# Two-layer graph attention on one core: the second layer's hub rows computed between the layers, 36 row tiles, waits by tile, a shorter norm pipeline

## The chip, the cores and the metric

The kernel runs on one core of one Trainium2 chip. The metric is device time in microseconds (us); lower is better. Three runs of the kernel before gave a median of 1045.44 us (1041.41 to 1046.57).

## The reference, cut to what matters

Eight batches of 2048 nodes with 64 features pass a two-layer graph attention net, are added to the input and normalised. An edge mask, the same for all batches and heads, decides which nodes attend to which.

```python
mask = graph + jnp.eye(N) > 0                    # N = 2048
h = jnp.einsum('bnc,hdc->bhnd', x, Wh)           # 4 heads, D = 64
out_h = softmax(where(mask, h @ h.T, -1e16)) @ h + bh     # layer 1, per head
z = leaky_relu(cat(out_h), 0.2)
h2 = jnp.einsum('bnk,dk->bnd', z, Wo)
out2 = softmax(where(mask, h2 @ h2.T, -1e16)) @ h2 + bo   # layer 2
z2 = leaky_relu(out2, 0.2)
y = layernorm(z2) * gamma + beta
return layernorm(x + y)
```

## The kernel before, in words

The mask is sparse: on average few neighbours, many only for low node numbers. The kernel (`fast_kernel`) therefore splits the nodes. The first 56 are hubs and attend densely to all nodes. The other 1992 form 166 sets of 12 nodes; each set gets a list of up to 128 nodes to which any of its members is linked, built from the mask (`make_keys`, `pick`). An indirect DMA on GpSimd (`gather`, L792) fetches the 128 rows of a set, 520 floats each, from a table in DRAM. All instructions are recorded in the order of the Python code; each engine runs its own in that order, and waits on semaphores for the others. No scheduler moves anything.

The work has three stages.

Stage one (to about 165 us) builds hub attention of layer 1, the key lists and table1.

Stage two is a loop over `i` in units of two sets (83 units) for layer 1. In one unit PE transposes the gathered rows of a later unit (`turn`, L512) into a PSUM tile that ScalarE copies to `xTg` (L1030), computes scores (L821), multiplies the weights by the values (`values`, L846), transposes the result (L863), projects it through the heads (L531), then through Wo into layer-2 columns (L880), and transposes these to rows (L890). `keep_own` (L885, L886) stores the columns as `own`, `keep_rows` (L894) stores rows and SyncE writes them to table2 (L897). The last unit's table2 rows are complete only at the end of the loop.

Stage three is layer 2, a loop over `u` in units of four sets (42 units, the last with two), on new pools `late` and `psum2`. Every gather of layer 2 reads table2, so none can begin before all its rows are written. 24 row tiles let the gathers of six units go ahead. In unit `u` the code issues, in this order: the scores of unit u+2 (`scores2`, L1133, and their exp on ScalarE, L1136); the value products of u (`values2`, L1165) into `op`, a PSUM tile for two units; on some units the value products of a hub block (L1299); the gathers of u+6; the jobs of running norms (`work_on(u, 0)`); the square roots of the norms (`roots`, L1239 and L1240); the weights of a hub block (L1285, L1288); the block-diagonal queries of u+3 (`spread_own`, L1124); the transposed scores of u+1 (L1144) and their mask (L1152); the transposes of u+4 (`turn2`, L512, and the copies L1320); the scores of a hub block (L1277); the remaining norm jobs (`work_on(u, 1)`).

The dense attention of the 56 hubs in layer 2 has 18 blocks (17 of up to 120 keys and one with the hubs themselves). Each costs a DMA of its rows (`hub_block`, L1267), eight score matmuls (L1277), a mask on VectorE (L1285), an exp on ScalarE (L1288) and 16 value matmuls (L1299). Four of them are in units -4 to -1, the other 14 in every second unit from 2 to 28.

A finished pair of units gives one norm (`norm`), 21 in all and one for the hubs. Its steps are: divide by the row sums (`first`, L1186 and L1188), leaky relu (L1193), sum (L1197), centre (L1202) and squares on ScalarE (L1204), sum of squares (L1213), root on ScalarE, scale, gamma and residual (`again`, L1217, L1221, L1222), then sum, centre, squares, sum of squares, root, scale again (`end`), and eight stores (L1248). The list that `norm` returns spreads them over eight units:

```python
return [([], [first, act, mean(0)]), ([centre(0)], []), ([var(0)], []), ([], [again, mean(1)]), ([centre(1)], []),
        ([], []), ([var(1)], []), ([end], [])]
```

At the end a flag is written which says whether the sums stayed in range; every engine loads it, and a general kernel would run if it were set.

Of the kernel before, what the change touches and what calls it, by code (L numbers as in the profile page):

```python
# [359 lines left out]
def fast_kernel(ctx: ExitStack, tc: tile.TileContext, x, adj, Wh, bh, Wo, bo, gamma, beta, out, flag):  # L360
# [54 lines left out]
    wnat = early.tile([P, H, C], F32, name="wnat")  # L415
    whT = early.tile([P, H * D], F32, name="whT")
    gram = early.tile([P, H, P], F32, name="gram")
    wos = early.tile([D, H * D], F32, name="wos")
# [68 lines left out]
    number = early.tile([P, 2, HALFN], U16, name="number")  # L487
# [81 lines left out]
    yh = early.tile([P, 2, 2 * HUB * H], F32, name="yh")  # L569
# [52 lines left out]
    def hub_later(t, new):  # L622
# [4 lines left out]
        def turn_back():  # L627
            pt = new(f"oth{t}", "T")
            for v in range(2):
                for k in range(2):  # L630
                    nc.tensor.transpose(pt[:, 0, (2 * v + k) * P:(2 * v + k + 1) * P], osb[:, v, k, :], ident)
            ot = held["oth", t] = work.tile([P, H, n], F32, tag="ot", name=f"otbh{t}")
            nc.scalar.copy(ot.rearrange("c h (w n) -> c h w n", w=8),
                           pt[:, 0, :].rearrange("c (w n) -> c w n", w=8)[:, :, :HV].rearrange("c w (n h) -> c h w n", h=H))
# [28 lines left out]
    keys = [early.tile([P, HALFN], F32, name=f"keys{k}") for k in range(2)]  # L663
    cand = early.tile([P, SEG * KEEP], F32, name="cand")
    best = early.tile([P, P], F32, name="best")
# [61 lines left out]
    def pick(r):  # L727
# [32 lines left out]
        def slots():  # L760
            nc.vector.tensor_copy(over[:, 2 * r + 1:2 * r + 2], best[:, P - 1:P])
            pb = two(f"pb{r}") if r == 0 else late_two(f"pb{r}")
            nc.tensor.transpose(pb[:, 0, :P], best, ident)
            for c, a, n in runs:
                nc.vector.tensor_copy(keysi[:, a:a + n], pb[:, 0, c:c + n])
            nc.vector.tensor_scalar(index[:, s0:s0 + n_r], keysi[:, s0:s0 + n_r], N - 1, None, OP.bitwise_and)
# [125 lines left out]
    def keep_rows(g, pr):  # L892
# [3 lines left out]
        for j in range(2):  # L896
            nc.sync.dma_start(out=dst[2 * g + j], in_=r[j * 48:(j + 1) * 48])  # L897
# [105 lines left out]

    begin = ExitStack()
    psum1 = begin.enter_context(tc.tile_pool(name="psum1", bufs=1, space=bass.MemoryType.PSUM))
# [4 lines left out]
    def late_two(name):  # L1010
        return one(name, "T")
# [5 lines left out]
    for i in range(-4, NG + 3):  # L1017
# [6 lines left out]
        cat = one(f"cat{i}", "C")  # L1024
# [3 lines left out]
        if 0 <= i + 2 < NG:  # L1028
            t = held["T", 1, i + 2] = work.tile([P, 2, 512], F32, tag="xTg", name=f"xTg{i + 2}", bufs=3)
            nc.scalar.copy(t, held.pop(("tp", i + 2)))  # L1030
# [6 lines left out]
        if 0 <= i + LOOK < NG and i > -3:  # L1037
            for j in range(2):
                gather(table1, 2 * (i + LOOK) + j, 1, rows_tile)
        if i + 6 < NG and i % 2 == 0 and i >= -2:  # L1040
            own_rows((i + 6) // 2)
        if 0 <= (i - 30) // 2 <= NV:
# [18 lines left out]
        if 0 <= i - 2 < NG:  # L1061
            second_maps(i - 2, cat[:, 0, 384:384 + GM])
        if 0 <= i - 3 < NG:
            second_rows(i - 3, cat[:GM, 1, 384:512])
        if 0 <= i + 4 < NG + NG % 2:
            columns(i + 4, cat)
        if 0 <= i - 2 < NG:
            keep_own(i - 2, cat[:, 0, 384:384 + GM])
        if 0 <= i - 3 < NG:
            keep_rows(i - 3, cat[:GM, 1, 384:512])  # L1070
# [5 lines left out]
        if 0 <= i + 3 < NG:  # L1076
            tp = held["tp", i + 3] = one(f"t{i + 3}", "T")
            turn(tp[:, 0, :], rows[1, 2 * (i + 3)])
# [3 lines left out]
        if 0 <= i + 3 < NG:  # L1082
            turn(tp[:, 1, :], rows[1, 2 * (i + 3) + 1])
    assert not picks and not pieces and not todo3 and done == NS
# [4 lines left out]
    late = ctx.enter_context(tc.tile_pool(name="late", bufs=2))  # L1089
    psum2 = ctx.enter_context(tc.tile_pool(name="psum2", bufs=1, space=bass.MemoryType.PSUM))  # L1090
# [3 lines left out]

    def rows2(name):
        return late.tile([P, Q, PW], F32, tag="rows", name=name, bufs=24)

    NU = (NS + 3) // 4
    sets = [list(range(4 * u, min(4 * u + 4, NS))) for u in range(NU)]
    for u in range(6):  # L1100
        for s in sets[u]:
            gather(table2, s, 2, rows2)
    bd = [late.tile([P, 4, Q, 32], F32, name=f"bd{k}", bufs=1) for k in range(3)]
    es2 = [late.tile([P, 2 * Q, 4, 32], F32, name=f"es2_{k}", bufs=1) for k in range(2)]
    esh = [late.tile([P, Q * 2 * HUB + 8], F32, name=f"esh{k}", bufs=1) for k in range(2)]
    ownb = late.tile([P, Q, 2, HUB], F32, name="ownb", bufs=1)
    nc.vector.memset(ownb, 0.0)
    for p in range(2):
        nc.vector.tensor_copy(ownb[half(p), :, p, :], ownh[half(p)].rearrange("c t (k n) -> c (t k) n", k=2))
    for t in bd:  # L1110
        nc.vector.memset(t, 0.0)
    for k in range(2):
        nc.vector.memset(esh[k][:, Q * 2 * HUB:], 1.0)
        nc.vector.memset(es2[k], 0.0)
    nc.vector.memset(es2[0][:, :, :, 24:], 1.0)
    linked = late.tile([P, NS, SET], U8, name="linked", bufs=1)
    nc.vector.tensor_scalar(linked, mask.rearrange("p s (k h) -> p s k h", h=H)[:, :, :, 0], 0.0, None, OP.is_equal)

    def spread_own(u):

        w = len(sets[u])
        for p in range(2):
            src = own[half(p), :, sets[u][0] * SET:(sets[u][0] + w) * SET]
            nc.scalar.copy(bd[u % 3][half(p), :w, :, 16 * p:16 * p + SET], src.rearrange("c q (k n) -> c k q n", k=w))  # L1124

    def scores2(u):

        w = len(sets[u])
        sp = psum2.tile([P, 4, P], F32, tag="S2", name=f"s2_{u}")
# [8 lines left out]
    def turn_scores(u):  # L1138
# [3 lines left out]
        te = psum2.tile([P, 4, P], F32, tag="S2", name=f"e2_{u}")  # L1142
# [11 lines left out]

    W2 = D + 2
# [15 lines left out]
    def norm(name, v, i, vals, dens, nb, store):  # L1171
# [3 lines left out]
        at = [v + 2, v + 6]  # L1175
# [48 lines left out]
        def end():  # L1224
# [3 lines left out]
        return [([], [first, act, mean(0)]), ([centre(0)], []), ([var(0)], []), ([], [again, mean(1)]), ([centre(1)], []),  # L1228
                ([], []), ([var(1)], []), ([end], [])]
# [12 lines left out]
    def norm_sets(v, op):  # L1242
        def store(y):
            for t in range(4):
                for a in range(2):
                    dst, w = nodes(t, v)(out, a)
                    p0 = t * 32 + a * SET
                    (nc.scalar if v == NV - 1 and a else nc.sync).dma_start(out=dst, in_=y[p0:p0 + SET].rearrange("p (f w) c -> p f (w c)", f=2)[:, :, :w * D])  # L1248
# [12 lines left out]

    def hub_block(b):
        t = rows["h", b] = late.tile([P, Q, PW], F32, tag="hrows", name=f"gh{b}", bufs=4)
        n = HUB if b == NHB else hub_sets(b)[1] * SET
        s0 = b * S10
        src = table2[:HUB, :] if b == NHB else table2[HUB:, :].rearrange("(k s) c -> s k c", s=NS)[s0:s0 + n // SET]
        nc.sync.dma_start(out=t.rearrange("n q c -> n (q c)")[:n], in_=src)  # L1267

    def hub_scores2(b):
        n = HUB if b == NHB else hub_sets(b)[1] * SET  # L1270
        sp = held["sh", b] = bank2(f"sh2_{b}", "T", 2)
        for q in range(Q):
            if b == NHB:
                keys = ownh[:, q // 2, q % 2 * HUB:(q % 2 + 1) * HUB]
            else:
                keys = own[:, q, b * S10 * SET:b * S10 * SET + n]
            nc.tensor.matmul(sp[:n, 0, q * 2 * HUB:(q + 1) * 2 * HUB], keys, ownb[:, q, :, :].rearrange("c p n -> c (p n)"),  # L1277
                             start=True, stop=True)

    def hub_lift2(b):  # L1280
        n = HUB if b == NHB else hub_sets(b)[1] * SET
        sp = held.pop(("sh", b))
        e = esh[b % 2]
# [150 lines left out]
```

## Time and profile before

| what | value |
| --- | --- |
| median of three runs | 1045.44 us |
| the profiled execution's own time | 880.76 us |
| its span, first to last instruction | 878.9 us |
| granted TensorE clock over the span | 0.951 |
| busy: PE, weight loads, DVE, ACT, POOL | 753.0, 661.2, 610.1, 514.4, 469.2 us |
| moved by DMA | 145.22 MB, 165 GB/s |

The profile is one execution. Its engines are PE (TensorE; PEld its weight loads), DVE (VectorE), ACT (ScalarE), POOL (GpSimd) and SP (SyncE, which issues DMAs; SPq is its queue). `L512` is a line of the kernel. A row of a timeline has the start, the time that the instruction took, engine, line and operation; in brackets stands how long the engine had been idle, and for what. A row of windows has a stretch of the span, its length, the busy time of each engine with its number of instructions, the granted TensorE clock, the share of DMA time and the rate. A gather's row on POOL is over before its data moves: it takes about 0.95 us, and the packets on its queue begin about 2 us after its start.

### The profile page before, as it was taken

What the parts mean: (1) busy time and instruction counts of PE and PEld (TensorE: products, weight loads), DVE (VectorE), ACT (ScalarE), POOL (GpSimd) and SP (SyncE); (2) the same over time, 40 slices, a digit from 0 to 9 for tenths busy, and PEclk for the clock granted to TensorE, in tenths of its full rate; (3) what the DMA queues carried; (4) which work ended last, traced back from release to release, by engine and by line L of the source; (5) the groups of instructions that cost most, each with busy time, mean ns of one, the idle gap of its engine ahead of it and who ended that gap; (6) DMA issues with size and microseconds to landing.
All of it is one profiled execution on the core that took longest, in us unless ns stands there. A gap on an engine that the chain in (4) does not pass through costs nothing.

```text
span 878.9 us, 42066 instructions
## 1 busy us (share of the span) xinstructions
PE 753.0 (86%) x18437; PEld 661.2 (75%) x18437; DVE 610.1 (69%) x1369; ACT 514.4 (59%) x961; POOL 469.2 (53%) x612
## 2 busy tenths in 40 slices
PE   1896777889999999999999999992999999998730
PEld 1664456778788999988999999971899999988720
DVE  3356983568888788877555555553258999998994
ACT  2342333556556667666766667651678888886821
POOL 5654141457444555655666666503777777777300
PEclk9998998999999999999999999995999999999965
DMA  8787451355434445655566665514888888888611
GB/s 167 238 218 213 129 146 48 83 142 160 109 100 118 112 125 159 162 169 153 160 168 173 160 166 162 134 28 114 246 266 253 275 275 267 266 252 242 172 46 35
DMA packets 81794, 145.22 MB, mean 165 GB/s; under 512 B 30146, under 2 KB 46466, under 8 KB 81602
## 3 DMA queue, kind: packets, MB, share of 16 engines
q0 software_dynamic: 26720, 88.55, 36.4%
q1 hardware_dynamic: 37842, 49.65, 18.7%
q10 hardware_dynamic: 17040, 4.25, 2.6%
q8 instruction: 147, 2.41, 1.1%
q14 instruction: 45, 0.37, 0.1%
HBM read 123.91 MB, written 18.48 MB: 162 GB/s over the span
## 4 chain that ended last, share of the span: by engine, by line
PE 63%; DVE 15%; DMA 7%; ACT 5%; issue 4%; SPq 3%; POOL 2%; DVEq 0%; ACTq 0%; POOLq 0%
PE t L512 11%; PE s L821 10%; PE o L846 10%; PE cat L806 6%; PE o L863 4%; PE cat L531 4%; PE cat L880 3%; PE s L1133 3%; PE o L1165 3%; PE cat L890 2%; DMA raw<-in_adj_dram 2%; SPq L1248 2%; PE sh L1277 2%; PE e L1144 2%; DMA g<-table,index 1%
## 5 line engine op out<-in xcount | busy, mean ns | idle before, releaser
L792 POOL DMA_INDIRECT g<-table,index x332 | 334.9, 1009 | 236.1 <-PE o L846 140.2
L512 PE MATMUL t<-ident,g 128*128 128x128 f32 x1328 | 182.3, 276 | 15.6 <-DMA g<-table,index 12.7
L512 PEld LDWEIGHTS t<-ident,g 128*128 128x128 f32 x1328 | 154.8, 142 | 20.0 <-issue 14.0
L826 DVE TENSOR_TENSOR e<-s,mask 128x768 f32<-128x768 f32 x83 | 79.4, 956 | 87.4 <-PE s L821 85.4
L518 ACT ACTIVATE z<-cat,bhp 128x192 f32<-128x192 f32 x166 | 60.8, 418 | 85.0 <-PE cat L531 85.0
L846 PE MATMUL o<-g,e 128*64 128x65 f32 x2656 | 97.5, 227 | 0.0
L821 PEld LDWEIGHTS s<-y,xTg 64*64 64x64 f32 x5312 | 85.2, 134 | 13.9 <-issue 13.7
L821 PE MATMUL s<-y,xTg 64*64 64x48 f32 x5312 | 95.5, 220 | 0.0
L846 PEld LDWEIGHTS o<-g,e 128*64 128x64 f32 x2656 | 85.8, 140 | 9.8
L1320 ACT COPY xTg<-t 128x1024 f32<-128x1024 f32 x83 | 80.3, 1017 | 18.1 <-PE t L512 17.3
L1030 ACT COPY xTg<-t 128x1024 f32<-128x1024 f32 x83 | 84.0, 1012 | 2.0 <-PE t L512 2.0
L833 ACT ACTIVATE e<-e,shifts 128x768 f32<-128x768 f32 x83 | 79.2, 955 | 2.1 <-DVE e L826 1.7
L812 ACT COPY y<-cat 128x384 f32<-128x384 f32 (+1 forms) x80 | 40.7, 508 | 64.0 <-PE o L863 40.1
L597 ACT ACTIVATE e<-e,shifts 128x896 f32<-128x896 f32 x32 | 33.4, 1042 | 73.0 <-DVE e L594 52.1
L680 POOL TENSOR_SCALAR a<-raw 120x1024 bf16<-120x1024 int32 (+1 forms) x34 | 38.2, 1125 | 65.1 <-DMA raw<-in_adj_dram 38.4
L806 PE MATMUL cat<-xo,gram 128*128 128x192 f32 (+1 forms) x320 | 65.6, 328 | 0.0
L853 DVE RECIPROCAL rall<-o 64x8 f32<-64x8 f32 x166 | 34.0, 205 | 42.0 <-PE o L846 40.7
L854 DVE TENSOR_TENSOR osb<-o,rall 128x512 f32<-128x512 f32 x83 | 57.4, 692 | 2.9
L1165 PE MATMUL o<-g,es 128*32 128x65 f32 x2656 | 49.1, 226 | 5.9 <-DVE y_s L1188 4.5
L806 PEld LDWEIGHTS cat<-xo,gram 128*128 128x128 f32 x320 | 53.7, 203 | 0.3 <-issue 0.2
L1165 PEld LDWEIGHTS o<-g,es 128*32 128x32 f32 x2656 | 46.1, 113 | 7.0 <-issue 4.9
L1133 PE MATMUL s<-xTg,bd 128*32 128x128 f32 x1328 | 45.4, 277 | 6.2 <-ACT bd L1124 3.5
(177 smaller groups left out, 1369.3 us busy)
## 6 DMA issues: line engine op xcount, KB each, us to landing
raw<-in_adj_dram SPq DMA_DIRECT2D x32, 480.0 KB
table<-xb SPq DMA_DIRECT2D x22, 256.0 KB
xr_s<-table SPq DMA_DIRECT2D x21, 256.0 KB
g<-table,index POOLq DMA_INDIRECT x332
table<-x SPq DMA_DIRECT2D x16, 260.0 KB
x<-in_x_dram ACTq DMA_DIRECT2D x32, 128.0 KB
table<-rowt SPq DMA_DIRECT2D x166, 24.4 KB
xb<-in_x_dram SPq DMA_DIRECT2D x164, 24.0 KB
```

The costliest lines, as they stand in the source:

```text
L512: nc.tensor.transpose(tp[:, q * P:(q + 1) * P], rows[:, q, 1:1 + P], ident)
L518: nc.scalar.activation(z[:, hp], cat[:, :, hp * n:(hp + 1) * n], AF.Identity, bias=bhp[:, hp:hp + 1], scale=1.0)
L792: nc.gpsimd.indirect_dma_start(out=t.rearrange("n q c -> n (q c)"), out_offset=None, in_=table, in_offset=bass.IndirectOffsetOnAxis(ap=ind ...
L806: nc.tensor.matmul(cat[:, k, 2 * GM:2 * GM + n], gram[:, g % 2 * 2 + k, :], held["x", g // 2][:, :n], start=True, stop=True)
L821: nc.tensor.matmul(sp[half(r), p, (q * 2 + j) * M:(q * 2 + j + 1) * M], xt[half(p), j, q, half(r)], y[half(p), (j * Q + q) * M:(j * Q + q ...
L826: nc.vector.tensor_tensor(e[:, :16 * M].rearrange("p (a q n) -> p a q n", a=2, q=Q), sp[:, :, :8 * M].rearrange("p a (q n) -> p a q n", q= ...
L833: nc.scalar.activation(e[:, :16 * M], e[:, :16 * M], AF.Exp, bias=shifts[:, 0:1], scale=1.0)
L846: nc.tensor.matmul(op[half(p), j, o0:o0 + K1], e[:, c0:c0 + 64], rw[j][:, q, sums(p)], start=True, stop=True)
L1030: nc.scalar.copy(t, held.pop(("tp", i + 2)))
L1133: nc.tensor.matmul(sp[q * 32:(q + 1) * 32, k, :], bd[u % 3][:, k, q, :], xt[:, s % 2, q, :], start=True, stop=True, tile_position=(0, q * 32))
L1165: nc.tensor.matmul(op[t * 32:(t + 1) * 32, f, k * W2 + p:k * W2 + p + K1], e[:, 2 * q + p, k, :], rw[:, q, sums(p)], start=(a == 0 and k = ...
L1320: nc.scalar.copy(t, tp)
```

## The change

It has five parts, named in its title and read here from the code.

1. The 18 hub blocks are numbered `k` with the hubs' own block first. Blocks 0 to 2 are computed in the last three full units of layer 1 (`hub_step(i - NG + 3, bank[0])`), steps 3 to 8 right after that loop, before the pools of layer 2 open, and steps 9 to 18 in units -3 to 5 of layer 2 (two in unit -3, then one per unit). The rows of blocks 0 to 7 are loaded in four late units of layer 1 on SyncE's queue into free row tiles of that stage; 8 to 13 after the loop into six tiles of their own, 14 to 17 as those come free. The tiles that layer 2 needs ready (`bd`, `es2`, `esh`, `ownb`, `linked`) lie in memory that stage one no longer needs (`share`), and are cleared and filled in layer 1's units from 60 on (`ahead_of_second`).
2. `psum1`, `late` and `psum2` are opened with `reuse_waits="tile"`. Two PSUM banks (`bank[0]`, `bank[1]`) live through both layers: layer 1's transposes go there and are copied by two ScalarE instructions in place of one; in layer 2 they hold the scores and the hub sums. Units after the last full one in layer 1 take other PSUM tiles for their projections.
3. 36 row tiles by number in place of a ring of 24: gathers run nine units ahead.
4. `turn2(u + 3)` stands first in unit `u` (it was `turn2(u + 4)` near the end), the hub step after the scores, `roots(u)` at the very end of the unit.
5. The norms go over five units, their roots one and three units after their start. The last pair's stores are dealt to three queues, and the last two units' table2 writes to two.

```diff
+    for k in range(3, 9):
+        hub_step(k, bank[0])
...
-        return [([], [first, act, mean(0)]), ([centre(0)], []), ([var(0)], []), ([], [again, mean(1)]), ([centre(1)], []),
-                ([], []), ([var(1)], []), ([end], [])]
+        return [([first], []), ([act, mean(0), centre(0)], [var(0)]), ([again], [mean(1)]), ([centre(1)], [var(1)]), ([], [end])]
...
-            nc.scalar.copy(t, held.pop(("tp", i + 2)))
+            for k in range(2):
+                nc.scalar.copy(t[:, k, :], bank[k])
...
+        if NG - LOOK <= i < NG - 1:
+            for j in range(2):
+                k = 2 * (i - NG + LOOK) + j
+                hub_block(k, rows_tile(f"gh{k}"))
...
+        if i >= 60 and i % 2 == 0 and ahead_of_second:
+            ahead_of_second.pop(0)()
...
+        if NG - 3 <= i < NG:
+            hub_step(i - NG + 3, bank[0])
...
-            nc.sync.dma_start(out=dst[2 * g + j], in_=r[j * 48:(j + 1) * 48])
+            (nc.scalar if j and g >= NG - 2 else nc.sync).dma_start(out=dst[2 * g + j], in_=r[j * 48:(j + 1) * 48])
...
-    late = ctx.enter_context(tc.tile_pool(name="late", bufs=2))
-    psum2 = ctx.enter_context(tc.tile_pool(name="psum2", bufs=1, space=bass.MemoryType.PSUM))
+    late = ctx.enter_context(tc.tile_pool(name="late", reuse_waits="tile", bufs=2))
+    psum2 = ctx.enter_context(tc.tile_pool(name="psum2", reuse_waits="tile", bufs=1, space=bass.MemoryType.PSUM))
...
-    for u in range(-4, NU + 7):
+    k = 9
+    for u in range(-3, NU + 5):
+        if u + 3 < NU:
+            turn2(u + 3)
         if 0 <= u + 2 < NU:
             scores2(u + 2)
+        for _ in range(2 if u == -3 else 1):
+            if k <= NHB + 1:
+                hub_step(k, bank2(f"sh{k}", "T", 2)[:, 0, :] if k <= NHB else None)
...
-        roots(u)
...
-        if u + 4 < NU:
-            turn2(u + 4)
...
         work_on(u, 1)
+        roots(u)
```

`hub_step` is new:

```python
def hub_step(k, sp):
    if k <= NHB:
        hub_scores2(k, sp)
        hub_lift2(k)
    if 0 < k <= NHB + 1:
        hub_values2(k - 1)
```

## The prediction

> **What bounds the kernel now.** I read the windows by stage first, then a timeline of layer 2, then POOL's own timeline, then the end. The windows cut the span at the end of layer 1, at the first value products of layer 2 and at the last:
>
> ```profile
> core 0: us, PE busy (x) PEld busy (x) DVE busy (x) ACT busy (x) POOL busy (x), PEclk, DMA share, GB/s
> 165.00:600.00 435.00, 418.79 (x11103) 376.33 (x11101) 301.74 (x779) 275.88 (x570) 234.99 (x313) 0.99 0.51 137
> 600.00:633.00 33.00, 19.02 (x221) 16.28 (x225) 10.90 (x24) 12.73 (x19) 21.11 (x22) 0.73 0.71 207
> 633.00:847.50 214.50, 197.24 (x5036) 181.17 (x5026) 185.86 (x336) 164.19 (x290) 146.86 (x145) 0.98 0.80 240
> 847.50:878.90 31.40, 0.19 (x2) 0.09 (x2) 18.88 (x36) 4.40 (x12) 0.00 (x0) 0.50 0.17 38
> ```
>
> Layer 1 is PE's: 419 of 435 us. Between the layers PE is busy 19 of 33 us at 0.73 of its clock. In layer 2 PE and DVE are both near full. In the last 31 us PE does nothing. Two units of layer 2, in order of PE:
>
> ```profile
> 714.28 0.93 PE L512 MATMUL t<-ident,g 128*128 128x128 f32 x7
> 715.14 1.08 PE L1133 MATMUL s<-xTg,bd 128*32 128x128 f32 x32
> 716.03 1.12 PE L1165 MATMUL o<-g,es 128*32 128x65 f32 x64
> 717.08 0.69 PE L1299 MATMUL oh<-gh,esh 120*64 120x65 f32 x16
> 717.70 0.66 PE L1144 MATMUL e<-ident,eT 128*128 128x128 f32 x4
> 718.20 1.91 PE L512 MATMUL t<-ident,g 128*128 128x128 f32 x16
> 720.34 1.09 PE L1277 MATMUL sh<-ownb,own 128*120 128x112 f32 x8 [0.23 <-ACT xTg L1320]
> 721.36 1.08 PE L1133 MATMUL s<-xTg,bd 128*32 128x128 f32 x32
> 722.25 1.13 PE L1165 MATMUL o<-g,es 128*32 128x65 f32 x64
> ```
>
> L1165 comes 6.22 us apart here, with one hub block between, and 4.30 us later again (726.55), without one. So a pair of units takes 10.5 us with its hub block and would take 8.6 us of PE without. The last rows are POOL's first gathers of layer 2, one from the loop, and the last stores:
>
> ```profile
> 605.49 0.96 POOL L792 DMA_INDIRECT g<-table,index  x1 [5.56 <-DVE ownb L1107]
> 606.76 0.95 POOL L792 DMA_INDIRECT g<-table,index  x1 [0.30 <-issue]
> ...
> 717.32 1.26 POOL L792 DMA_INDIRECT g<-table,index  x1 [0.30 <-PE o L1165]
> ```
>
> ```profile
> 855.31 19.64 SPq L1248 DMA_DIRECT2D out_dram<-y_s  x28
> ```
>
> A gather costs POOL 0.95 us and a gap of 0.30, so four cost 5.0 us a unit, against PE's 5.25. The gap never grows in layer 2, so POOL is never idle there: it takes from 605.49 to 822.80 for 166 gathers, 1.317 us each. SP still issues stores at 875, five us after the last of DVE.
>
> [...] of the 99 gathers between 650 and 780 us, 33 took over 1.0 us; 64% of these lay beside DVE's L1202, which reads two SBUF tiles, and only 24% of the rest did. So fewer stalls of PE don't speed POOL. [...] Here the first gather stands at 605.49 and PE's first transpose of it at 611.09, 5.6 us later. [...] a store costs SP 0.37 us here.
>
> **The sum's own time.** The profiled execution took 880.76 us: 878.9 of span and 1.9 around it. The median of the runs is 164.7 us longer. [...] a slower PE clock in the timed runs would explain it; a constant would too. I work out the sum for the profile, then carry it over both ways.
>
> **The change, part by part.**
>
> *Hub steps 0 to 2 in layer 1.* PE gets 1.09 + 2 x (1.09 + 0.69) = 4.7 us in the last full units, where it waits for copies of ScalarE (0.7 to 0.9 us, several times from 583 on). I take +2. The projections of the last units no longer share PSUM with the rows being read: two waits of 0.70 us go, -1.4. Their DMAs, eight of 0.78 us on SP, stand before table writes of the same units; 6 us over four units of 5 hide in SP's waits (L897 waits for DVE's rows); exposed, at most +2.
>
> *Clearing and filling in advance* (nine fills and clears of 0.07 to 1.2 us on DVE, six bd copies of 0.35 us on ACT) leaves the 605-611 stretch. In layer 1 DVE is busy 28.5 of the 50 us before 550, so 21 us of it free hide them; with that cover gone they are about 7 us. POOL's first gather then waits for table2 alone, not by way of ownb, which DVE clears: SP goes on at 604.63, when the last write has landed, so 605.49 - 604.63 = -0.9; halving the last writes between queues -0.5.
>
> *Layer 1's copies in two* cost ACT some 0.2 us a unit (L1030 takes 1.01 for 1024 columns, L518 0.42 for 192, so 0.2 is fixed); nothing excludes that the earlier half frees its bank sooner, but PE has no gap there to fill. ACT is busy 276 of 435 us, 1.9 us free a unit: 0. With that cover gone it is 0.2 x 83 = 17 us. Layer 1 and the start together: -1, from -4 to +5.
>
> *Steps 3 to 8 in the gap.* One step is scores 1.09, the way to DVE 0.2, mask 0.62 (the next scores need the bank back): 1.95 with the values beside the mask. Six are 12 us, 19 at half clock. They begin at 600.4 and end at 612 to 619; the fourth gather lands at about 615. So they cost nothing or up to 4, and PE's idle time takes them. [...] The first value products of layer 2 need gathers 0 to 15, which POOL issues 15 x 1.27 = 19 us after the first, as before. So 633 stays: 0, from -2 to +4.
>
> *The loop.* PE's hub work there falls from 14 blocks to about five. What is late next is POOL: unit u needs the gathers of u+3, and 150 gathers lie between those of unit 0 and the last. The floor is 1.25 x 150 = 187.5 us; contention adds, as DVE's work is unchanged; I take 1.30 (the row shows 1.25, the stage's mean is 1.317): 195. Before, units 0 to 38 took 834.47 - 633.26 = 201.2. That is -6, from -14 to +3. The other limits: PE 8.6 a pair, DVE 9.25 (the pair's rows from 714.42 to 724.93 less 0.64 idle and 0.61 hub mask), against 10.4 for POOL. The 36 tiles remove no wait, as gathers waited for no tile. Transposes first is a rotation of a cycle: 0, except that the hub scores no longer wait 0.23 and 0.47 for a copy, within POOL's cover. A new wait is `roots(u)` at the unit's end: it waits for the variance of the same unit, and the copies of the next unit's transposes are queued behind it on ACT, and PE's scores behind those. Mask 0.66, two variances 1.3, roots 0.6, copies 1.95, exp 0.7, transposes 0.66 make an even unit of 5.9, an odd one 4.3: 10.2 a pair, under 10.4. Hidden, barely.
>
> *The end.* After the last value products DVE ran 27 full-size instructions; by the new list 17 remain (1 + 2 + 4 + 2 + 3 + 2 + 1 + 1 + 1). Ten at 0.66 us are -6.6. SP's queue is empty earlier and the eight stores go to three queues: SP ended 5.5 us after DVE, I take 2 to 2.5; POOL's two need about 1.25 each. -3. The end: -10, from -13 to -5.
>
> Sum: -1 + 0 - 6 - 10 = -17, a profile of about 864 us.
>
> *To the median.* As a constant, -17 gives 1028. [...] -33 gives 1012. I take the middle, -23: **1022 us**, likeliest between 1008 and 1033.
>
> **The rivals.**
>
> *POOL runs free* (0.15): with tile-wise waits, contention nearly gone and nine units ahead, the loop goes at DVE's 9.25 a pair. 38 units take 176, not 201: -25, the end -10: -36, and -42 with a slow PE: 1003. For it: POOL never waits. Against: its own 1.25 a gather forbids 9.25 before the 36 in hand are used up.
>
> *The change moves work but no end* (0.10): POOL keeps 1.317, hub steps delay the first gather by 4 to 5 us, and the end gives only 6: 1043. For it: the gather stream is the same in both. Against: 27 DVE rows at the end.
>
> *Slower by the new ACT wait* (0.08): if the squares are late too, DVE waits for them (0.63) and for the roots (0.6) in each pair, ACT and PE behind it. Each pair over 10.4 costs 20.5 x the excess; it turns the sign at 1.1 us a pair, and at 1.7 the loop is 35 us longer: 1045 - 23 + 35 = 1057. For it: 10.2 is near 10.4. Against: squares stand before the wait for L1144.
>
> **The numbers.** Forecast 0.67. Half a per cent, 5 us, is about what a measurement can tell from no change, as the runs spread by that. Faster by more: 0.67 + 0.15 = 0.82; same 0.10; slower 0.08. The range takes in half of the first and second rivals and leaves 0.2 out: 1003 to 1041.
>
> **What would show it.** In the profile after: PE busy with L1065 rows between 600 and 613; the first gather by 605 and the 166th start near 818; POOL's gap still 0.30; units 10.0 to 10.5 a pair; last value products at 840, last DVE row 15 us on, span 864. Wrong if POOL's gap grows (something else binds), if layer 1's unit exceeds 5.0 us, or if ACT waits for L1296's variance by over 1 us a pair.

## The result, and the profile after

The changed kernel takes 1031.21 us (median of four runs, 1028.61 to 1034.0), the kernel before 1046.01 us beside it: a ratio of 0.9869 with a 95% interval of 0.9835 to 0.9904. It is faster by 1.3%, about 15 us; the forecast was 1022.

One fact has to stand ahead of everything else. The runs of this study fell on several chips, and they are not alike. The same kernel before took a median of 1046.6 and 1046.1 us on two of them, and 879.1 and 881.9 us on two others. The first profile of before (880.8 us) is of the second, quicker kind; the times beside it, and the profile of the changed kernel, are of the slower kind. So the 165 us between the profile and the median, which the prediction put down to PE's clock or to a constant, are the difference between these two kinds. (Each of the four chips served at one time only, so a chip's own pace isn't told apart from something that lasted through its runs.) A second profile of before, on a slower chip, can be set against the changed kernel; one of the changed kernel on a quicker chip against the first profile of before.

The windows below all have the same four cuts: first to last score product of layer 1; to the first value product of layer 2; to the last; to the end. On the slower chips, before (columns as in the fence after it):

```profile
158.10:614.20 456.10, 440.19 (x11267) 393.44 (x11270) 304.87 (x776) 284.28 (x573) 237.46 (x315) 0.99 0.48 132
614.20:679.60 65.40, 34.38 (x408) 26.42 (x403) 17.35 (x42) 17.22 (x30) 24.70 (x28) 0.71 0.44 126
679.60:1008.50 328.90, 251.66 (x5026) 208.14 (x5014) 186.12 (x335) 162.50 (x290) 140.07 (x142) 0.90 0.55 152
1008.50:1040.00 31.50, 0.48 (x14) 0.14 (x6) 19.20 (x36) 4.40 (x12) 0.00 (x0) 0.50 0.17 39
```

and the changed kernel:

```profile
core 0: us, PE busy (x) PEld busy (x) DVE busy (x) ACT busy (x) POOL busy (x), PEclk, DMA share, GB/s
158.60:624.80 466.20, 444.33 (x11281) 395.20 (x11282) 311.32 (x789) 290.94 (x662) 242.50 (x316) 1.00 0.49 133
624.80:714.20 89.40, 47.83 (x649) 40.90 (x642) 17.17 (x39) 22.28 (x35) 35.25 (x40) 0.71 0.53 153
714.20:1005.90 291.70, 212.62 (x4760) 178.86 (x4762) 186.82 (x333) 155.28 (x280) 127.37 (x130) 0.94 0.56 150
1005.90:1032.20 26.30, 0.53 (x17) 0.18 (x6) 14.84 (x29) 3.44 (x9) 1.24 (x2) 0.50 0.14 33
```

The gain is no sum of small gains: layer 1 lost 10 us, the way to layer 2 lost 24, the loop of layer 2 won 37 and the end 5. The changed kernel on a quicker chip, same cuts:

```profile
core 0: us, PE busy (x) PEld busy (x) DVE busy (x) ACT busy (x) POOL busy (x), PEclk, DMA share, GB/s
152.00:596.60 444.60, 423.54 (x11279) 379.62 (x11281) 309.48 (x789) 286.29 (x662) 242.28 (x315) 1.00 0.51 139
596.60:645.70 49.10, 42.96 (x649) 36.97 (x641) 17.12 (x39) 22.36 (x35) 24.76 (x29) 0.93 0.61 181
645.70:717.70 72.00, 60.93 (x1509) 54.58 (x1509) 53.83 (x103) 48.83 (x89) 55.59 (x54) 1.00 0.84 248
717.70:865.60 147.90, 119.78 (x3262) 109.85 (x3257) 131.38 (x232) 106.02 (x192) 95.69 (x87) 0.97 0.72 208
865.60:892.40 26.80, 0.54 (x18) 0.19 (x6) 14.85 (x29) 3.44 (x9) 1.23 (x2) 0.50 0.14 32
```

There the loop is cut once more, after six pairs. The first profile of before has for these five stretches 433.7, 47.5, 61.7, 152.2 and 31.7 us. So on a quicker chip: layer 1 +11, the way +1.6, six pairs +10.3, the other pairs -4.3, the end -4.9, together +13.5. (The medians of the runs there say +11.)

Now the rows that answer to those of before. Line numbers are one higher up to the hub blocks; then L1065, L1074, L1077 and L1088 are a hub step's scores, mask, exp and values, L1218, L1221, L1229 and L1237 the scores, their exp, the turned scores and their mask, L1248 the value products, L1363 the copies, L1321 the roots. PE between the layers on the slower chip:

```profile
645.79 0.69 PE L1088 MATMUL bank<-gh,share 120*64 120x65 f32 x16
650.57 1.94 PE L1065 MATMUL bank<-share,own 128*120 128x112 f32 x8 [4.08 <-DVE share L1074]
...
677.37 1.94 PE L1065 MATMUL bank<-share,own 128*120 128x112 f32 x8 [21.55 <-issue]
...
682.21 0.27 PE L1088 MATMUL bank<-gh,share 120*64 120x65 f32 x1 [2.26 <-issue]
683.61 0.27 PE L1088 MATMUL bank<-gh,share 120*64 120x65 f32 x1 [1.14 <-issue]
...
696.69 1.09 PE L1065 MATMUL sh<-share,own 128*120 128x112 f32 x8
697.84 0.69 PE L1088 MATMUL bank<-hrows,share 120*64 120x65 f32 x16
```

One stop of 21.55 us, then single matmuls 1.4 us and more apart, all with "issue", that is, without a wait that the profile shows; from 697 on 16 value matmuls take 0.69 us again. DVE and ACT stop as well, ACT once for 26.1 us. The waits of DVE's masks between 642 and 694 us (total, number, longest) are put to "remote", though the profile, which models the ends of matmuls, has the scores before the longest one over at 652.5 us and the mask at 676.7:

```profile
DVE share L1074 <- remote: 47.7, 3, 26.2
```

POOL over this time, and its first gather of the loop:

```profile
655.16 0.95 POOL L793 DMA_INDIRECT rows<-table,index  x1 [0.30 <-issue]
...
686.51 0.95 POOL L793 DMA_INDIRECT rows<-table,index  x1 [0.31 <-issue]
714.90 0.95 POOL L793 DMA_INDIRECT rows<-table,index  x1 [27.45 <-PE o L1248]
```

POOL issues its 36 gathers in a row, from 642.60 to 687.5; PE gets little done for as long and 6 us more. On the quicker chip PE goes on beside the same row of gathers:

```profile
615.25 1.09 PE L1065 MATMUL bank<-share,own 128*120 128x112 f32 x8 [0.17 <-DVE share L1074]
616.27 0.69 PE L1088 MATMUL bank<-gh,share 120*64 120x65 f32 x16
617.13 1.09 PE L1065 MATMUL bank<-share,own 128*120 128x112 f32 x8 [0.17 <-DVE share L1074]
```

Windows laid over the two rows of gathers say it in one number each: PE is busy 11.85 of 50.8 us on the slower chip, 41.62 of 45.5 on the quicker, POOL 34.2 and 34.5. The loop on the slower chip, one unit:

```profile
835.62 1.13 PE L1248 MATMUL o<-rows,share 128*32 128x65 f32 x62
838.04 0.66 PE L1229 MATMUL bank<-ident,eT 128*128 128x128 f32 x4 [1.29 <-ACT eT L1221]
838.53 1.91 PE L513 MATMUL t<-ident,rows 128*128 128x128 f32 x16
841.12 0.92 PE L1218 MATMUL bank<-xts,share 128*32 128x128 f32 x25 [0.67 <-DVE share L1237]
842.31 0.36 PE L1218 MATMUL bank<-xts,share 128*32 128x128 f32 x4 [0.27 <-issue]
...
842.56 1.13 PE L1248 MATMUL o<-rows,share 128*32 128x65 f32 x62
```

6.9 us from L1248 to L1248, on average 14.4 a pair with the other unit, where the quicker chip takes 9.99. The last stores, on SP's queue on the slower chip:

```profile
1019.43 6.63 SPq L1331 DMA_DIRECT2D out_dram<-y_s  x11
```

SP is through at 1026, the span at 1032: three queues moved SP's end, not the end.

### The profile page after: what moved, and what is told of

It reads as the page before. It is cut to its first block, busy times and chain, and to the rows that moved or that the text cites. A ratio compares the mean times of both kernels' runs of the same rounds, so it can differ in the third digit from the quotient of the medians.

```text
span 1032.2 us, 42364 instructions
## 1 busy us (share of the span) xinstructions
PE 813.3 (79%) x18437; PEld 693.3 (67%) x18437; DVE 616.0 (60%) x1369; ACT 521.4 (51%) x1042; POOL 467.7 (45%) x614
## 4 chain that ended last, share of the span: by engine, by line
PE 59%; DVE 15%; issue 13%; ACT 6%; DMA 4%; POOL 1%; SPq 1%; another core or an unknown queue 0%; DVEq 0%; POOLq 0%; ACTq 0%
PE s L822 10%; PE o L847 9%; PE bank L513 7%; PE t L513 6%; PE cat L807 4%; DMA raw<-in_adj_dram 4%; PE cat L532 3%; PE o L864 3%; PE bank L1218 3%; PE cat L881 2%; ACT xts L1363 2%; PE bank L1229 2%; PE o L1248 2%; PE cat L891 2%; PE bank L1088 1%
## 5 line engine op out<-in xcount | busy, mean ns | idle before, releaser
L793 POOL DMA_INDIRECT g<-table,index x166 | 170.7, 1029 | 213.9 <-PE o L847 172.7
L793 POOL DMA_INDIRECT rows<-table,index x166 | 161.5, 973 | 164.1 <-PE o L1248 97.8
L1363 ACT COPY xts<-t 128x1024 f32<-128x1024 f32 x83 | 79.8, 1011 | 53.2 <-PE t L513 44.3
L513 PE MATMUL bank<-ident,g 128*128 128x128 f32 x664 | 100.3, 274 | 0.3 <-ACT otbh L634 0.2
L1218 PE MATMUL bank<-xts,share 128*32 128x128 f32 x1328 | 58.8, 288 | 45.7 <-DVE share L1237 26.1
L513 PE MATMUL t<-ident,rows 128*128 128x128 f32 x664 | 89.3, 280 | 5.2 <-issue 4.4
L1124 ACT COPY xTg<-bank 128x512 f32<-128x512 f32 x166 | 89.2, 597 | 0.5 <-PE bank L513 0.5
L513 PEld LDWEIGHTS t<-ident,rows 128*128 128x128 f32 x664 | 76.6, 144 | 14.1 <-issue 13.3
L513 PEld LDWEIGHTS bank<-ident,g 128*128 128x128 f32 x664 | 79.9, 142 | 2.9 <-ACT otbh L634 0.5
L1218 PEld LDWEIGHTS bank<-xts,share 128*32 128x32 f32 x1328 | 40.0, 113 | 61.7 <-issue 39.0
```

The lines of the kernel that those rows point to most:

```text
L513: nc.tensor.transpose(tp[:, q * P:(q + 1) * P], rows[:, q, 1:1 + P], ident)
L793: nc.gpsimd.indirect_dma_start(out=t.rearrange("n q c -> n (q c)"), out_offset=None, in_=table, in_offset=bass.IndirectOffsetOnAxis(ap=ind ...
L1124: nc.scalar.copy(t[:, k, :], bank[k])
L1218: nc.tensor.matmul(sp[q * 32:(q + 1) * 32, k, :], bd[u % 3][:, k, q, :], xt[:, s % 2, q, :], start=True, stop=True, tile_position=(0, q * 32))
L1363: nc.scalar.copy(t, tp)
```

## The experiments

"Changed kernel" is the kernel after. The kernels under one heading ran on the same chip, and each ratio is to before on it.

### On a slower chip (before 1046.6 us)

**A second profile of before**, unchanged.

> The kernel before, unchanged, for a second profile. Theory: the first profiled execution (880.8 us) was an unusual one, and this one shows the pace of the runs, 1041 to 1048 us, with the lost 165 us as stalls of PE for which the trace shows no reason, as in the trace of the changed kernel (a unit of the first layer 5.3 to 5.5 us instead of 5.0, and stalls of 1 us and more in the second layer), at a granted clock near 1.0. Rival: a lower granted clock, [...] through the whole span, as the prediction supposed. Second rival: profiled executions of this kernel are always quick, near 880 us; then the two kernels' profiles cannot be set against each other.

One run, 1041.86 us, its windows above. The theory held for the pace (a unit of layer 1 takes 5.34 us, the median, against 5.00 on the quicker chip). The lower clock through the whole span fell: the granted clock is 0.99 in layer 1 and 0.90 in the loop, where it drops to 0.50 once in each of ten pairs with a hub block (below). The loss against the quicker chip is 22 us in layer 1, 18 between the layers and 115 in the loop.

**Six units ahead.**

```
-    for u in range(9):
+    for u in range(6):
...
-        for s in sets[u + 9] if 0 <= u < NU - 9 else []:
+        for s in sets[u + 6] if 0 <= u < NU - 6 else []:
```

> The changed kernel (1031 us) with the gathers of the second layer six units ahead instead of nine, so 24 gathers stand in the queues between the layers instead of 36. Theory: the 36 gathers crowd what the stalled engines wait for between the layers (one stall of PE of 21.6 us), and with 24 that stall is shorter by a third, about 7 us: 1022 to 1027 us. Rival: the stall has nothing to do with the number of gathers, and the larger stock of tiles is worth nothing either: 1029 to 1033 us. Third: the stock of 36 is what lets the loop run past the stalls, and without it the loop is 5 to 15 us longer: 1036 to 1046 us.

1033.72 us, ratio 0.9888 (0.9842 to 0.9935): no change, and no test either. POOL runs on as far as tiles are free, so all 36 were filled in one row all the same, to 689.7 us.

**The old list of the norms** in the changed kernel: `at = [v + 2, v + 6]`, the list over eight units, `roots` after the first jobs.

> The changed kernel with the norms spread over eight units again, as before; all else as changed. Theory (the term of the prediction for the end, of which the new list is -6.6 us): about 1031 + 7 = 1036 to 1041 us. Rival: the new list costs in the loop, by the wait for the variance of its own unit on ACT, what it saves at the end: 1029 to 1033 us. Third: it costs more than it saves, 1020 to 1027 us.

1028.3 us, ratio 0.9855 (0.9806 to 0.9904). The first theory fell: the end is 6 us longer (32.3 against 26.3), the loop 10 us shorter (281.4 against 291.7). What the short list gives at the end it takes in the loop; the two totals can't be told apart, as the intervals overlap.

**The waits by tile alone**, in before.

```
-    tc.tile_pool(name="psum1", bufs=1
+    tc.tile_pool(name="psum1", reuse_waits="tile", bufs=1
...
-    tc.tile_pool(name="late", bufs=2
+    tc.tile_pool(name="late", reuse_waits="tile", bufs=2
...
-    tc.tile_pool(name="psum2", bufs=1
+    tc.tile_pool(name="psum2", reuse_waits="tile", bufs=1
```

> The kernel before (1046 us) with only the pools' waits tile by tile, in the PSUM of both layers and in the SBUF of the second. Theory: 0, as no wait of the trace before is one on a whole pool except at the start of the second layer: 1043 to 1049 us. Rival: tiles that come free one by one let PE and ACT run further ahead past stalls, 5 to 15 us faster: 1031 to 1041 us.

1044.0 us, ratio 0.9996 (0.9970 to 1.0022): nothing, as the theory had it.

### On a quicker chip (before 879.1 us)

**24 row tiles** in the changed kernel, six units ahead.

> The changed kernel (1031 us) with 24 row tiles instead of 36, the gathers six units ahead. In the earlier try with six units the gathers still ran on into the 36 tiles, as nothing but a free tile holds POOL back (37 in a row between 645 and 690 us), so it tested nothing. Theory A (PE gets almost nothing done while POOL issues gathers back to back; the hold goes with the gathers in a row): the row of gathers between the layers is 24 instead of 36, 12 x 1.25 = 15 us shorter, and 12 more gathers in the loop give back 12 x 0.6 = 7: 1020 to 1027 us. Theory B (the stock of 36 is what shortened the loop by 37 us): 1040 to 1060 us. Neither: 1029 to 1033 us.

896.36 us, ratio 1.0206 (1.0164 to 1.0248). The numbers were meant for a slower chip, so it tests nothing of PE's stop between the layers. What it shows is that this variant is no gain here. Its way to the first products is 46.7 us and its loop 222.5, against 49.1 and 219.9 with 36 tiles; seven of its later pairs take 10.6 to 11.5 us where 36 tiles give 9.99, as POOL can no longer be run ahead of: PE waits 12.7 us for gathers between 756 and 850.

**Plain DMAs on SP in place of the gathers of layer 2**, 128 consecutive rows each.

> The changed kernel with the gathers of the second layer replaced by plain DMAs on SP, each of 128 consecutive rows of the same table into the same tile; it leaves out the indexing (the rows are not those of the graph), and keeps bytes, tiles and their order. Theory A (POOL's issuing of gathers holds PE): the stop between the layers and the stalls of the loop go, units of 10 to 10.5 us a pair as in the quick profile of before: 920 to 960 us. Theory C (the data of the gathers, not their issuing, hold PE): no less than 1010 us, with the same stalls without a shown reason. Theory D (the chip's PE is slow in these runs for a reason of its own): 1020 to 1035 us.

The wrong rows leave the range that the program tests at its end, so the general kernel runs after this one, and the run's 7233 us say nothing; the trace up to 890 us does. The loop takes 226 us (659.5 to 885.6). Since PE's long stop beside the gathers is there on slower chips alone, theories A and C stay untold apart.

**The gathers of the loop left out.** The time, 7213 us, has the same reason.

> The changed kernel with the 130 gathers of the second layer's loop left out (units from the tenth on read what the first 36 gathers brought). Theory A and C alike: the loop is PE's or DVE's alone, 190 to 205 us instead of 292, so 930 to 945 us, with the stop between the layers unchanged. Theory D (PE slow for its own reason): the loop stays over 260 us, so over 1000 us.

Its loop, cut after six pairs:

```profile
648.70:718.70 70.00, 59.92 (x1506) 53.92 (x1508) 53.56 (x103) 48.75 (x89) 9.21 (x10) 1.00 0.31 94
718.70:861.80 143.10, 117.88 (x3263) 108.55 (x3258) 131.24 (x232) 106.02 (x192) 0.00 (x0) 0.98 0.21 49
```

213.1 us without a gather, longer than the 190 to 205 of theories A and C, 219.9 with all of them, and 9.99 us a pair in steady state in both. So in the changed kernel on a quicker chip POOL isn't what sets the pace. Of the 7 us between the two, 5 are one pair, of 15.0 us, in which PE stops twice (below); this run has no such pair.

**Hub steps 3 to 8 back in the loop.**

```
-    for k in range(3, 9):
-        hub_step(k, bank[0])
...
-    k = 9
+    k = 3
     for u in range(-3, NU + 5):
```

> The changed kernel with hub steps 3 to 8 taken out of the place between the layers and put into the loop, one a unit as the steps after them. Theory A: what stands between the layers is done while PE is held by the gathers anyway, so those six steps cost there little, and in the loop they cost 1.8 us of PE and a wait for the copies of up to 3 us each, as in before: 6 x 1.8 to 6 x 4.8, 1041 to 1060 us. Rival (the steps only stood in the way of the first transposes, and the loop has room for them): 1015 to 1027 us.

The rows of blocks 2 to 13 are now loaded after layer 1, into the six tiles that blocks 8 to 13 had. 900.11 us, ratio 1.0237 (1.0195 to 1.0280). Against the changed kernel's 1.0127 (1.0081 to 1.0173, next run) the intervals are apart: six steps cost about 1.1% (10 us) more in the loop than between the layers, 1.6 us a step, a little under the theory.

### On another quicker chip (before 881.9 us)

**The changed kernel itself.**

> The changed kernel, unchanged, beside runs of before on the same chip. So far before took 1046 us on one chip and 879 us on another. On the slower one the changed kernel took 1031 us. If this runs on a chip where before takes about 1046 us: 1027 to 1035 us again. On one where before takes about 879 us, theory E (layer 1 costs 10 us more on both chips, the loop gains only where PE is held by the gathers, the end gains 6): like its two variants there, 890 to 902 us, slower than before. The prediction's own sum: 864 us there.

892.84 us, ratio 1.0127 (1.0081 to 1.0173): slower than before by 1.3% here. Theory E's range held, the prediction's 864 didn't.

**Fills out of layer 1, two lists of norms.**

```
-        if i >= 60 and i % 2 == 0 and ahead_of_second:
-            ahead_of_second.pop(0)()
...
-        if NG - 3 <= i < NG:
-            hub_step(i - NG + 3, bank[0])
-    for k in range(3, 9):
-        hub_step(k, bank[0])
+    ahead_of_second.pop(0)()
+    for k in range(9):
+        hub_step(k, bank[0])
+        ahead_of_second.pop(0)()
...
-        at = [v + 1, v + 3]
+        short = v == NU - 1
+        at = [v + 1, v + 3] if short else [v + 2, v + 6]
```

> The changed kernel with two edits. The fills, the clearing, the bd copies and hub steps 0 to 2 stand after the first layer instead of in its last units, and the norms of all pairs but the last are spread over eight units as before, the last over five. Theory E: layer 1 gets back the 6 to 7 us that these jobs cost its even units from the 64th on, the end keeps its 6 us, and the loop gets back what the wait for the variance of its own unit costs (10 us where before takes 1046): 12 to 18 us less than the changed kernel, 1013 to 1020 us or 880 to 888 us by chip. Rival (DVE's fills were hidden, and the short list costs nothing in the loop): within 3 us of the changed kernel. Third (what leaves layer 1 stands in full between the layers, and delays the first products by 6 us): 5 to 10 us less than the changed kernel.

893.05 us, ratio 1.0135 (1.0099 to 1.0172): no gain, though its parts show. Its windows, same cuts, from the first on:

```profile
154.00:593.00 439.00, 421.24 (x11267) 378.34 (x11270) 303.69 (x776) 284.54 (x655) 238.56 (x315) 1.00 0.52 140
593.00:649.80 56.80, 46.73 (x661) 39.42 (x651) 23.37 (x52) 24.30 (x41) 31.91 (x36) 0.88 0.65 190
649.80:716.10 66.30, 60.39 (x1509) 54.24 (x1511) 48.87 (x93) 49.13 (x87) 51.27 (x50) 1.00 0.84 247
716.10:856.50 140.40, 119.93 (x3262) 109.65 (x3255) 130.55 (x233) 110.58 (x194) 92.27 (x85) 0.99 0.74 215
```

Layer 1 gets 5.6 us back, the way to layer 2 gives 7.7 for it; the loop is 13.2 us shorter than in the changed kernel (5 of them by a pair in which PE stops there, below), and 7 shorter than in before; but the end is 31.9 again. The short list for the last pair alone leaves 27 full-size DVE rows after the last product, as in before, where the changed kernel has 20.

### On another slower chip (before 1046.1 us)

**Two lists, the short one for the last two pairs, and hub steps 13 to 18 on every second unit.**

```
+        short = v >= NU - 3
...
-            if k <= NHB + 1:
+            if k <= NHB + 1 and (u < 0 or u % 2 == 0):
```

> The changed kernel with two edits: the norms of all pairs but the last two are spread over eight units as before, those two over five; and the hub steps 13 to 20 take every second unit of the loop instead of each. From the traces where before takes 880 us: the pairs of steady state go from 9.99 to 9.79 us (16 of them, -3), the first six, which carried two hub blocks each, from 12.3 to about 10.6 while two more pairs take up blocks (-8), the end stays 27. So 892.8 - 11 - 3 = 876 to 884 us there, against 892.8 for the changed kernel and 880 for before. Where before takes 1046: 1031 less 3 to 10 us, 1018 to 1028. Rival (the hub blocks cost the same wherever they stand, and the old list's gain is lost by the end of the second to last pair): 890 to 894, or 1028 to 1033.

(The last step is the 18th, not the 20th.) 1029.53 us, ratio 0.9843 (0.9802 to 0.9883): the rival's number. The loop is 277.8 us, 14 less than in the changed kernel, the end 33.5, 7 more. Its five pairs with one hub block take 14.5 to 16.9 us (15.7 on average), nine without that follow 14.1.

**The short list for the last two pairs in before**, nothing else.

> The kernel before with one part of the change alone, and that only at the end: the norms of the last two pairs over five units, all other norms over eight. By the traces the change shortens the end from 31.7 to 26.8 us, and this takes over nothing else: 874 to 877 us where before takes 880, 1040 to 1042 where it takes 1046. Rival (the short lists of two pairs crowd DVE in the last units of the loop and give back what the end gains): no difference.

1045.49 us, ratio 0.9986 (0.9962 to 1.0011): no difference, the end 31.1 us.

No version was shown to beat before on both kinds of chip. The two best on a slower one, the old list (0.9855) and the spaced steps (0.9843), weren't timed on a quicker one, and their intervals overlap with that of the changed kernel. A shorter row of gathers in the changed kernel on a slower chip wasn't tried, nor hub blocks back in its loop there.

## Why the prediction was right, and where it was wrong

The direction held where the times were taken, by another sum than the one worked out. That sum, -17 to 864 us, belongs to the quicker chips, and there it is +13.5 between the profiles.

*Hub steps 0 to 2, clearing and filling: "-1, from -4 to +5".* Failed: +10 to +11 on both kinds. "21 us of it free hide them" was the false step. Free time of DVE over 50 us says nothing of an instruction put in the middle of a unit's chain. On the quicker chip, DVE in a unit with a fill, and PE in the next:

```profile
531.06 0.91 DVE L1098 MEMSET share<- 128x1024 f32 x1 [0.16 <-PE cat L807]
531.89 0.49 DVE L524 SCALAR_TENSOR_TENSOR z<-z 128x384 f32<-128x384 f32 x1
```

```profile
533.83 0.56 PE L532 MATMUL cat<-otb,whT 64*64 64x96 f32 x16 [0.47 <-ACT otb L871]
```

The 0.91 us fill stands ahead of L524, L886 and L895, ACT's copies wait for those, PE for ACT: a unit of 5.77 instead of 5.00. Taking fills and steps out of layer 1 gave 5.6 us. The other 5 are a balance: in the run without fills, units 26 to 28, 38 to 40, 50 and 52, 62 and 74 take 7.9 us more than in before, the first 26 units 2.3 less. In those late units PE stops amid a line, for up to 1.5 us and with "issue" as the reason; the slower chip has longer units at the same places (more on these stops below). The steady unit is 5.00, so the copies in two cost nothing in it, as said. The earlier first gather of layer 2, the other part of this term (-0.9 and -0.5), came: it starts 17.9 us after the end of layer 1 instead of 19.8.

*Steps 3 to 8 between the layers: "0, from -2 to +4".* Right on the quicker chip: 1.88 us a step (1.95 expected), the stretch +1.6. On the slower, +24: in before PE gets little done until 668, 34 us from the first of 24 gathers, with 36 gathers for 51, which is +16 (12 more at 1.25 us are 15); from there to the first products it takes 21 us instead of 12, +9; -1 stands ahead of it. A row of gathers had no price in the prediction, as the profile that it read has no such stop.

*The loop: "-6, from -14 to +3".* On the quicker chip +6.0. The -6 is there: leaving out the first three pairs, those with the hubs' own norm and one with stops, a pair takes 9.90 us on average where before took 10.34; times fifteen this is -6.6, and steady state is 9.99, "10.0 to 10.5" foretold. Two things ate it. The "about five" blocks left stand in the first three pairs, two to a pair, where PE is the bound (8.6 + 2 x 1.78 = 12.2; the pairs take 12.9, 13.2 and 10.9 instead of 9.8, 9.9 and 10.5): +6.8. The prediction counted the blocks and didn't look where they fall. And in one pair PE stops twice amid a line, without a wait that the profile shows, +5:

```profile
750.54 0.43 PE L1248 MATMUL o<-rows,share 128*32 128x65 f32 x14 [1.91 <-issue]
...
757.60 0.31 PE L1248 MATMUL o<-rows,share 128*32 128x65 f32 x4 [2.38 <-issue]
```

The variants have such stops in other pairs or not at all. The times of DMA packets in the traces tell more than the timeline does: all 53 stops of PE of over 0.6 us amid a line without a wait that the profile shows, from 150 us to the end of layer 2 in the seven traces of quicker chips, end 1.2 to 1.7 us after a packet of the instruction queue (q8, "instruction" on the page, 16 KB) has landed, and these packets come about 5.4 us apart. The two above end 1.41 and 1.29 us after one, and the first of these packets took 1.86 us, where the median is 0.99. So PE seems to wait there for its own instructions. That is argued from times; no run tests it. (The hubs' own norm, two pairs of 12.2 us, only moved.) Nor is POOL the reason for 9.99. A gather took 1.084 us beside the loop, not 1.0:

```profile
L793 POOL DMA_INDIRECT rows<-table,index x130 | 140.9, 1084 | 39.6 <-issue 19.5 <-DMA rows<-table,index 7.6 <-PE bank L1229 7.0
```

against 0.947 for the 37 before it, while DVE is busy 28% of the time, and 1.017 in before's layer 2. Why they are longer here than in before isn't shown, as DVE is busy 87% beside these gathers and 85% beside those; nor does any run test whether DVE's L1202 lengthens a gather, which the prediction read from their overlap in time. It matters little, since 36 tiles in stock let the pairs run ahead of POOL.

*`roots`: "Hidden, barely".* It was not. On the quicker chip ACT waits for the variance and does the roots before the copies:

```profile
731.44 0.31 ACT L1321 ACTIVATE var<-var,shifts 128x16 f32<-128x16 f32 x1 [0.42 <-DVE var L1296]
...
731.90 1.91 ACT L1363 COPY xts<-t 128x1024 f32<-128x1024 f32 x2
```

and behind them PE and DVE wait, in every pair:

```profile
734.45 0.66 PE L1229 MATMUL bank<-ident,eT 128*128 128x128 f32 x4 [1.40 <-ACT eT L1221]
```

```profile
732.03 0.69 DVE L1300 TENSOR_TENSOR y_s<-y_s,var 128x512 f32<-128x512 f32 x1 [0.62 <-ACT var L1322]
```

That ring was worked out as 10.2 and is 9.99; it was put below a POOL limit of 10.4 that the stock of tiles removed. With the old list, and the roots at their old place, a pair takes 9.79, the first six 11.05 on average: 8 us of loop without the stops, and 10 on a slower chip. It is the rival "slower by the new ACT wait", at a quarter of its price. The sign named for it, a wait for the variance of over 1 us a pair, didn't show: in steady state it is 0.42 us.

*The end: "-10, from -13 to -5".* -4.9 and -5.2. DVE's rows give -4.7 (22.2 to 17.5 us from the last product to the last row), not -6.6: 20 full-size rows stand there where the prediction counted 17, so seven went and not ten. The stores give 0.2 instead of 3, since 9.3 us lie after DVE's last row, 9.5 in before. And it wasn't to be had alone: with the short list for one pair or two the end stayed at 31 to 33.5 us; it came with the short list for all pairs, which costs the loop 8 to 10. Numbers of pairs between weren't tried.

*To the median: "As a constant", -17, or with a slower PE clock, -33.* Both failed. The -33, like the rival's -42 "with a slow PE", rests on the author's estimate of that clock, which no trace shows: in the second profile of before it is 0.99 in layer 1 and 0.90 in the loop. What the slower chips lose is not one factor: 22 us of a layer 1 of 456, 115 of a loop of 329. A pair that holds a hub block takes 18.2 us there in before, one without in the changed kernel 14.4, 3.8 apart. Windows over these ten pairs, in before and in the changed kernel:

```profile
759.05:940.90 181.85, 141.63 (x2567) 115.40 (x2567) 95.66 (x170) 85.67 (x152) 79.14 (x80) 0.88 0.55 154
799.70:943.80 144.10, 102.64 (x2330) 85.84 (x2334) 93.76 (x163) 79.88 (x142) 76.82 (x79) 0.98 0.66 180
```

PE is idle 40 us in the first and 41 in the second; it is busy 39 us longer. The ten blocks' own work, 1.78 us each, is 18 of that. About the same again is the clock: an estimate from the granted clocks of these windows, 0.88 and 0.98, is 0.12 x 181.85 - 0.02 x 144.10 = 19. In before PE waits for a copy ahead of each block's scores, 0.2 us on the quicker chip and far longer here (between 690 and 1000 us; total, number, longest), and its matmuls after the wait are slow:

```profile
PEld sh L1277 <- ACT xTg L1320: 30.6, 12, 3.6
```

```profile
821.93 1.94 PE L1277 MATMUL sh<-ownb,own 128*120 128x112 f32 x8 [3.03 <-ACT xTg L1320]
823.80 1.94 PE L1133 MATMUL s<-xTg,bd 128*32 128x128 f32 x32
```

In the first profile of before, where the granted clock is 1.00 from 717 to 723 us, the same rows take 1.09 and 1.08 us. The ten pairs hold ten stretches of 3.4 to 6.8 us at a granted clock of 0.50, and each begins within 1.5 us of a block's scores; the changed kernel has two in its ten pairs. The prediction had this wait as "0.23 and 0.47", "within POOL's cover". Ten pairs freed of block and slow clock are 38 us, as much as the whole gain of the loop; the first five pairs lose 6, the last ones win 5. That the wait brings the slow clock is read from their order in time; no run tests it. What took the wait away, the block's leaving or the new order of the unit, no run on a slower chip separates; in the new order a pair with a block is 1.6 us longer than one without there (the run with spaced steps). The waits by tile gave nothing alone and the old norms make the loop shorter still, so neither is the cause. More row tiles are an unlikely one: between 690 and 1000 us of before PE waits for a gather's rows once, 0.7 us, while POOL waits 110 us for value products.

Right by the wrong sum, then, and by luck: -23 was put between two guesses, -17 and -33 (their middle is -25), and neither describes a slower chip. Between the two profiled executions on slower chips the sum is -37 (loop) + 24 (way to layer 2) + 10 (layer 1) - 5 (end) = -8; the medians say -15.

## What to carry to other kernels

Check first that the profile and the times have one pace: if they differ by 19%, get a profile at the pace of the times before any sum. An instruction moved into "free" time costs what stands behind it in its unit, not its share of a busy window: here a fill of 0.91 us made a unit of 5.00 us one of 5.77. A shorter pipeline at the end, which draws its steps together in every unit, was paid for in the loop; of moved steps, count which units they fall in, not how many are left.

## What the runs showed that was not expected

One kernel took 879 and 882 us on two chips of one type and 1046 and 1047 on two others, 19% more, with a granted clock of 0.99 in layer 1 on both kinds. On the slower ones PE gets little done while POOL issues gathers in a row (11.85 us busy in 50.8), and in the loop a pair takes 14.4 instead of 9.99 us. ACT and DVE stand still beside these gathers too (2.68 and 2.11 us busy in the same 50.8), and no run shows on what. That the gathers cause the stops is argued from their times, in two kernels (24 and 36 in a row), and not shown by taking them away on such a chip. Nor are these the stops that follow instruction packets: in the 51 us of the long row one such packet starts, at 692.4. What differs is open, but it isn't the speed of single packets or gathers: a packet of the gathers takes 0.16 us, the median, on both kinds, and a gather between the layers 0.95.
